# When the loads of the last stage are asked for: one in each of 17 steps, or one in each quarter of the last steps

## The chip, the cores and the metric

The kernel runs on one core of a Trainium2 chip (trn2). The metric is the device time of one execution in microseconds (us); the figure before is the median of three runs. All data is float32.

## The reference

The input x has 16 images of 64 channels of 128 × 128. Four layers follow, each of the form x = x + f(gn(x)), where gn is a group norm over groups of two channels:

- layer 0: the Gram matrix of an image's channels, applied to the image, then a product with a 64 × 64 matrix;
- layer 1: the absolute values of two Sobel-like 3 × 3 filters, added;
- layer 2: a shift of half of the channels by one column, then a 3 × 3 convolution of 64 to 64 channels with a bias;
- layer 3: a 3 × 3 convolution and a 1 × 1 convolution (done as one here), then a batch norm over all 16 images, a leaky ReLU and a clip to 0..255.

The batch norm matters for the shape of the kernel: its mean and variance need layer 3's product y of every image, so no element of the result can be finished before the last y is known.

## The kernel before, in words

Images go through a chain of four stages that work on different images at the same time: an image is cut into NS = 8 chunks (8 rows of each of its halves), and each stage works on one chunk in a step. A step has four quarters, q = 0 to 3. The loop runs over `steps` = 164 steps (0 to 163). `Gram` computes an image's Gram matrix; `Front` does layers 0 and 1; `Layer2` and `Layer3` do the convolutions. `starts` says how far the stages lie apart: for image b, Front's chunk 0 is at step 15 + 8b, Layer2's at 25 + 8b, Layer3's at 35 + 8b. For the last image (b = 15) Front ends at step 143, Layer2 has its last products in step 152, and Layer3 runs from step 155 (`last_one`) to 162, with a last store in 163. Layer3 of image 14 fills steps 147 to 154.

The order of instructions on each engine is the order in which the code records them (`InOrder`); no scheduler moves them. SP (SyncE) issues nearly all loads and stores, so an SP instruction that waits holds up all SP instructions behind it. Each SP load or store also waits, in the built program, until the one issued eight places earlier has landed.

What the steps around the change do on SP, in this order: in q = 1 Layer3 stores the y of the step before (`y_d<-y`, four stores of 128 KB), then Layer2 loads its chunk after the next (`v<-x_d`, six pieces, twelve for an image's last chunk); in q = 2 Layer2 stores its result, called x3 (`x_d<-x`, four stores of 128 KB). The names in the profile leave numbers out: y_d is layer 3's product in DRAM, x_d is layer 2's result (`x3_d`) or layer 1's (`x2_d`).

Buffers that later steps need: y has 2 (`ring`, tag "y"), x3 has NS + 2 = 10, v2 (layer 2's input) has 3. In q = 2 VectorE copies the product out of PSUM into y and adds the bias part c, `y<-two,c`; this needs a y buffer whose stores, two steps older, have landed. POOL copies the row differences d2 of layer 2 into a shifted twin, `qd<-d` (two pairs in a step, each a DMA issued by POOL on its own queue); TensorE reads them in q = 2 and q = 3. In layer 3 the twin is copied by ScalarE.

After the loop the end begins: the statistics (`mv`, `me_bn`, `var_bn`, `sc`, `sh`) are made from the sums, and then for each of 128 parts (512 KB of y, 512 KB of x3 and 512 KB of result each) ScalarE does the ReLU in place, VectorE the clip and the addition, and SP the store. The loads of a part are recorded by `fetch`, which takes two tiles of 128 × 1024 from a list of free places, `room`. Once the stages no longer need their tiles, `rest` and `slices` add them to `room`: `slices` cuts xw into 8 places, xh into 3, and d2 and its twin into one each; `rest` adds the tiles of a pool's tag. So some parts are fetched while the last steps still run, and three more after the loop:

```python
            yt, rt = room.popleft(), room.popleft()
            sp.dma_start(yt, whole(y_d[b], q))
            sp.dma_start(rt, whole(x3_d[b], q))
```

The fetched parts are the first ones, those of images 0 and 1, which were written long before. In the end, each part's places go back to `room`, and the next part is fetched into them.

Of the kernel before, what the change touches and what calls it, by code (L numbers as in the profile page):

```python
# [21 lines left out]
NS = HH // R  # L22
# [86 lines left out]
def tile_kernel(ctx: ExitStack, tc: tile.TileContext, x, cw_h, w2_t, b2, wbin_t, w1_t, b1, gamma, beta, consts, out):  # L109
# [142 lines left out]
    def tick():  # L252
        for c in list(chains):
            if next(c, chains) is chains:
                chains.remove(c)
# [608 lines left out]
    def run(stage, b, i, q):  # L864
        if 0 <= b < B and stage.first <= i <= stage.last:
            if (stage, b) not in live:
                live[stage, b] = stage(b)
            live[stage, b].at(i, q)
# [9 lines left out]
    last_one = NS * (B - 1) + starts[0][1]  # L878
# [5 lines left out]
    room, loaded = deque(), deque()  # L884
# [4 lines left out]
    def rest(pool, tag, shape, bufs, n=None):  # L889
        for m in range(bufs if n is None else n):  # L890
            t = pool.tile([P] + shape, F32, tag=tag, name=f"end_{tag}_{len(room)}", bufs=bufs)
            while len(t.shape) > 2:
                t = t.rearrange("p a b c -> p (a b) c" if len(t.shape) == 4 else "p a b -> p (a b)")
            room.append(t[:, 0:N])

    def slices(t, n):
        room.extend(t[:, j * N:(j + 1) * N] for j in range(n))
# [3 lines left out]
    def fetch():  # L901
        n = fetched[0]
        if n < len(parts):
            b, q = parts[n]
# [3 lines that stand above are left out]
            loaded.append((yt, rt))  # L908
            fetched[0] += 1

    for step in range(steps):
        for q in range(4):
            for b in range(B):

                i = step - starts[2][1] - NS * b
                if 0 <= i < NS and q in (0, 2):
                    live[Front, b].sobel(i, f"first of {q}")
                if q == 3:
                    run(Layer2, b, step - starts[1][1] - NS * b, "first of 3")
            for stage, at in starts:  # L920
                for b in range(B):
                    run(stage, b, step - at - NS * b, q)
            if q == 3:
                for b in range(B):
                    run(Layer2, b, step - starts[1][1] - NS * b, "last of 3")
            for b in range(B):
                at, n = pace[b]
                for m in range(n):
                    v = 4 * n * (step - at) + n * q + m
                    run(Gram, b, v // 4, v % 4)  # L930
            tick()

            if step == last_one and q == 0:
                slices(xw.rearrange("p w c t -> p (w c t)"), 8)
                slices(xh.rearrange("p a j w -> p (a j w)"), 3)
                rest(xin, "x", [R, W], 2)
                rest(xin, "xr", [C // 8, W], 3)
                rest(work, "u", [R + 1, W + 2], 2)
                rest(work, "e", [R, W + 2], 1)
                rest(ring, "v2", [(R + 1) * W + 2], 3)  # L940
                for t in (diffs["d2"], twins["d2"]):
                    slices(t.rearrange("p n j w -> p (n j w)"), 1)
            if step >= last_one and q == 2:

                n = 3 if step == last_one else 1 if step < last_one + NS - 2 else 0
                rest(ring, "x3", [2, CP, W], NS + 2, n)
            if step >= last_one and len(room) > 1:
                fetch()
    while chains:
        tick()  # L950
# [80 lines left out]
```

## Time and profile before

| | |
|---|---|
| median of three runs | 2827.53 us (2825.04 to 2830.61) |
| the profiled execution's own time | 2829.05 us |
| its span, from the first to the last instruction | 2827.3 us |
| TensorE, VectorE, ScalarE, GpSimd busy | 2241.5, 2200.4, 2120.5, 884.3 us |
| first ReLU of the end | at 2381.2 us of the span |
| end loads before the statistics | 16 parts (32 loads of 512 KB), first issued at 2299.6 us |
| DRAM read and written | 346.23 and 268.44 MB |

The page gives the busy time of each engine, then the span in 40 slices of 70.7 us with the busy share of each engine in tenths, the granted TensorE clock (PEclk) and the DMA engines' share and GB/s. The trace behind it gives the instructions of an engine in order of time: start, duration, instruction, and in square brackets how long the engine was idle before it and what ended that. Nearly all instructions carry line 73, that of the helper which records them, so they are told apart by the names of their tiles. Tiles that `rest` adds are called end_x, end_v and so on; xw, xh, d and qd are the same tiles as in the steps. A busy TensorE row has about 68 matmuls in 14 us in these steps.

### The profile page before, as it was taken

The page shows a single profiled execution, that of the slowest core. Times are in us where ns is not written, and L with a number is a line of the kernel's source. Part 1 is how long each engine was busy: PE and PEld are TensorE (multiplying, and loading weights), DVE is VectorE, ACT ScalarE, POOL GpSimd, SP SyncE. Part 2 cuts the span into 40 slices and gives each one's busy share as a digit, 9 for nine tenths or more (in the row PEclk, how much of TensorE's full clock was granted, in tenths as well). Part 3 has the DMA queues.
Part 4 walks back from the last instruction along what each step waited for, and adds up shares of the span by engine and source line. Part 5 has one row for each costly group of instructions (what it writes and reads, how often), then busy time and mean ns, then how long its engine had stood idle before and what let it go on. Part 6 is the DMA issues. An engine that isn't in the chain of part 4 may idle for free. (4 is left out here: it accounts for less than half of the span.)

```text
span 2827.3 us, 46297 instructions
## 1 busy us (share of the span) xinstructions
PE 2241.5 (79%) x14772; PEld 1157.1 (41%) x14772; DVE 2200.4 (78%) x3758; ACT 2120.5 (75%) x3171; POOL 884.3 (31%) x1326
## 2 busy tenths in 40 slices
PE   4568899999999999999999999999999995000000
PEld 2333444545453535363646363566666641000000
DVE  3999999898989898989898989999996434333332
ACT  4666779888888888888888888998997666333332
POOL 1035433343434343434343434454444300000000
PEclk8678999999999999999999999999999997555555
DMA  6788978888888888888888877888877668999999
GB/s 166 192 219 227 235 199 237 213 232 205 229 209 224 213 221 215 220 216 223 215 221 216 220 183 191 207 207 213 208 209 186 156 201 285 419 420 420 420 420 391
DMA packets 688880, 685.95 MB, mean 243 GB/s; under 512 B 61744, under 2 KB 590144, under 8 KB 688640
## 3 DMA queue, kind: packets, MB, share of 16 engines
q1 hardware_dynamic: 662656, 614.42, 73.7%
q0 software_dynamic: 24576, 68.12, 9.8%
q8 instruction: 119, 1.95, 0.3%
q14 instruction: 121, 0.99, 0.1%
q10 hardware_dynamic: 1408, 0.46, 0.1%
HBM read 346.23 MB, written 268.44 MB: 217 GB/s over the span
## 5 line engine op out<-in xcount | busy, mean ns | idle before, releaser
L73 PE MATMUL two<-d,w 128*64 128x508 f32 (+2 forms) x2560 | 894.2, 588 | 5.8 <-DVE d L73 5.8
L73 PE MATMUL two<-d,wi 128*64 128x508 f32 (+3 forms) x1536 | 620.1, 577 | 0.0
L73 POOL DMA_DIRECT2D qd<-d x512 | 269.8, 529 | 870.8 <-issue 318.4
L73 PE MATMUL two<-qd,pk 128*64 128x512 f32 (+1 forms) x1024 | 520.3, 589 | 3.2 <-DMA qd<-d 2.1
L73 POOL TENSOR_SCALAR edges<-v,co 64x8 f32<-64x8 f32 x512 | 348.8, 681 | 357.9 <-ACT v L73 248.7
L73 PEld LDWEIGHTS two<-d,w 128*64 128x64 f32 x2560 | 305.3, 136 | 285.5 <-issue 194.7
L73 PE MATMUL po<-x,abd 128*64 128x512 f32 x1024 | 369.8, 629 | 61.6 <-ACT xh L73 60.6
L73 DVE TENSOR_TENSOR d<-v 128x512 f32<-128x512 f32 (+1 forms) x512 | 345.9, 678 | 75.3 <-issue 36.0
L73 PE MATMUL one<-v,w 128*64 128x508 f32 (+2 forms) x1600 | 394.7, 578 | 0.0
L73 PE MATMUL one<-v,wi 128*64 128x508 f32 (+3 forms) x1536 | 391.4, 593 | 0.0
L73 ACT COPY qd<-d 64x512 f32<-64x512 f32 x512 | 315.3, 616 | 30.1 <-DVE d L73 23.7
L73 DVE SCALAR_TENSOR_TENSOR e<-e 128x1032 f32<-128x1032 f32 (+1 forms) x256 | 312.7, 1222 | 0.0
L73 ACT ACTIVATE xh<-po,co 128x128 f32<-128x128 f32 (+1 forms) x480 | 275.1, 621 | 40.8 <-PE po L73 38.8
L73 DVE SCALAR_TENSOR_TENSOR y<-two,c 128x1024 f32<-128x1024 f32 x128 | 155.8, 1217 | 132.0 <-ACT v L73 44.2
L73 PEld LDWEIGHTS two<-d,wi 128*64 128x64 f32 x1536 | 195.7, 136 | 145.2 <-issue 97.7
L73 POOL TENSOR_SCALAR v<-v,kc 128x9 f32<-128x9 f32 x256 | 249.7, 988 | 11.9
L73 PEld LDWEIGHTS one<-v,w 128*64 128x64 f32 x1600 | 171.9, 137 | 159.3 <-issue 97.5
L73 ACT ACTIVATE v<-x,co 128x512 f32<-128x512 f32 (+2 forms) x368 | 234.9, 704 | 0.0
L73 PEld LDWEIGHTS one<-v,wi 128*64 128x64 f32 x1536 | 163.0, 139 | 154.2 <-issue 110.1
L73 ACT ACTIVATE u<-u 128x1024 f32<-128x1024 f32 x128 | 135.5, 1058 | 96.7 <-DVE u L73 96.3
L73 DVE SCALAR_TENSOR_TENSOR u<-xh 128x1170 f32<-128x1170 f32 x128 | 175.5, 1371 | 12.2 <-ACT xh L73 9.8
L73 PEld LDWEIGHTS po<-x,abd 128*64 128x64 f32 x1024 | 110.8, 140 | 174.3 <-ACT xh L73 93.1
(154 smaller groups left out, 3476.0 us busy)
## 6 DMA issues: line engine op xcount, KB each, us to landing
xr<-in_x SPq DMA_DIRECT2D x128, 512.0 KB, 6.6
x<-in_x SPq DMA_DIRECT2D x256, 256.0 KB, 4.2
x_d<-u SPq DMA_DIRECT2D x512, 128.0 KB, 3.6
y_d<-y SPq DMA_DIRECT2D x512, 128.0 KB, 4.3
x_d<-x SPq DMA_DIRECT2D x496, 128.0 KB, 2.5
qd<-d POOLq DMA_DIRECT2D x256, 130.0 KB, 3.1
qd<-d POOLq DMA_DIRECT2D x256, 129.8 KB, 3.6
v<-x_d SPq DMA_DIRECT2D x448, 72.1 KB, 3.0
```

Of the source, the lines that this page charges most:

```text
L73: return self.tc.keep_in_program_order(call(*args, **kwargs))
```

## The change

Two things move. The tiles that Front and Gram leave (xw, xh, x, xr, u and e, 19 places) are put into `room` at step `last_one - NS` = 147 instead of `last_one` = 155; the tiles of Layer2 (v2 and d2 with its twin, 5 places) still at 155, and the x3 tiles as before. And `fetch` is called once in a step, in q = 3, from step 147 on, instead of in every quarter from step 155 on. Both wait for two free places (`len(room) > 1`).

```diff
-            if step == last_one and q == 0:
+            if step == last_one - NS and q == 0:
                 slices(xw.rearrange("p w c t -> p (w c t)"), 8)
                 slices(xh.rearrange("p a j w -> p (a j w)"), 3)
                 rest(xin, "x", [R, W], 2)
                 rest(xin, "xr", [C // 8, W], 3)
                 rest(work, "u", [R + 1, W + 2], 2)
                 rest(work, "e", [R, W + 2], 1)
+            if step == last_one and q == 0:
                 rest(ring, "v2", [(R + 1) * W + 2], 3)
                 for t in (diffs["d2"], twins["d2"]):
                     slices(t.rearrange("p n j w -> p (n j w)"), 1)
...
                 n = 3 if step == last_one else 1 if step < last_one + NS - 2 else 0
                 rest(ring, "x3", [2, CP, W], NS + 2, n)
-            if step >= last_one and len(room) > 1:
+
+            if step >= last_one - NS and q == 3 and len(room) > 1:
                 fetch()
```

The order of the parts and the places they go to stay the same, and so do the instructions of every engine other than SP and their order. On SP each of the 32 loads has another place in the order: the first fourteen stand between the x3 stores and the next y stores of steps 147 to 153, the rest behind the y stores of steps 154 to 162. The three fetches after the loop stay where they are.

## The prediction

> **What bounds the kernel now.** I read the page's 40 slices first (one slice is 70.7 us), then the busy time of each engine in stretches of 14 us around the steps that the change touches, then VectorE's and SP's instructions in order of time, then the chain of waits. The slices give the stages:
>
> ```profile
> PE   4568899999999999999999999999999995000000
> ...
> DMA  6788978888888888888888877888877668999999
> ```
>
> TensorE bounds the stepped part up to slice 34; the DMA engines bound the six slices after it, which are the end's loads and stores. Between them the stretches show a short piece where neither rule holds:
>
> ```profile
> 2232.00:2246.00 14.00, 14.00 (x68) 8.88 (x66) 5.65 (x11) 9.27 (x16) 4.87 (x10) 1.00 0.62 162
> ...
> 2316.00:2330.00 14.00, 14.00 (x61) 4.95 (x58) 4.88 (x8) 10.56 (x20) 0.00 (x0) 1.00 1.00 351
> 2330.00:2344.00 14.00, 11.50 (x42) 4.12 (x41) 2.44 (x4) 9.09 (x16) 0.00 (x0) 0.88 1.03 364
> 2344.00:2358.00 14.00, 10.58 (x39) 4.27 (x37) 2.44 (x4) 7.59 (x13) 0.00 (x0) 0.88 0.98 336
> 2358.00:2372.00 14.00, 13.73 (x58) 4.48 (x56) 4.88 (x8) 9.48 (x16) 0.00 (x0) 1.00 0.42 130
> ```
>
> The columns are PE, PEld, DVE, ACT, POOL (us busy, instructions), clock, DMA share, GB/s. At 2232 (step 149) TensorE is full and DMA has 38% free. From 2316 the DMA engines are full, and at 2330 TensorE loses time for the first time. Who holds it is seen in VectorE's copy of layer 3's product, one for each step:
>
> ```profile
> 2319.59 1.22 DVE L73 SCALAR_TENSOR_TENSOR y<-two,c 128x1024 f32<-128x1024 f32 x1 [5.38 <-ACT v L73]
> ...
> 2327.42 1.22 DVE L73 SCALAR_TENSOR_TENSOR y<-two,c 128x1024 f32<-128x1024 f32 x1 [5.38 <-PE two L73]
> ...
> 2338.32 1.22 DVE L73 SCALAR_TENSOR_TENSOR y<-two,c 128x1024 f32<-128x1024 f32 x1 [8.46 <-DMA y_d<-y]
> ...
> 2350.82 1.23 DVE L73 SCALAR_TENSOR_TENSOR y<-two,c 128x1024 f32<-128x1024 f32 x1 [10.06 <-DMA y_d<-y]
> ...
> 2360.07 1.23 DVE L73 SCALAR_TENSOR_TENSOR y<-two,c 128x1024 f32<-128x1024 f32 x1 [6.81 <-DMA end_x<-y_d]
> ...
> 2367.89 1.22 DVE L73 SCALAR_TENSOR_TENSOR y<-two,c 128x1024 f32<-128x1024 f32 x1 [5.38 <-ACT v L73]
> ...
> 2375.72 1.22 DVE L73 SCALAR_TENSOR_TENSOR y<-two,c 128x1024 f32<-128x1024 f32 x1 [5.39 <-issue]
> ```
>
> The last one is step 162, so these are steps 156 to 162. Three of them wait for a store of y (the third row names an end load, but the four DMA waits in the order of instructions are those of y's four stores): y has two buffers, so step 158 writes where step 156's y still lies. The store is late because SP issues it after eight end loads:
>
> ```profile
> 2324.32 0.43 SPq L73 DMA_DIRECT2D end_xr<-y_d  x1
> 2324.79 0.43 SPq L73 DMA_DIRECT2D end_xr<-x_d  x1
> 2325.27 0.43 SPq L73 DMA_DIRECT2D end_u<-y_d  x1
> 2325.74 0.70 SPq L73 DMA_DIRECT2D end_u<-x_d  x1
> 2326.76 4.48 SPq L73 DMA_DIRECT2D y_d<-y  x4
> ```
>
> The y of 2319.59 is stored from 2326.76, 6 us after it was ready, and lands behind full queues. Lastly the chain of waits, where the end starts:
>
> ```profile
> 2381.01 0.17 DVE sh L73
> 2381.18 0.03 issue
> 2381.21 1.25 ACT xw L73
> ...
> 2388.27 9.33 DMA out<-xh
> ```
>
> The batch statistics, which need the last y, gate the end at 2381.2; from 2388 on the chain is loads and stores of some 10 us each.
>
> **What the Trainium skill says.** (1) DMA: Bandwidth & Descriptors, section Anatomy of one DMA: "DMA engines do not wait on semaphores"; the issuing sequencer does. The trace agrees: SP's own waits name landings of xh, end_x, end_v and others between 2304 and 2358 (2.8 us for xh alone); while SP waits, the y store behind it is not issued. (2) Same page, section Queues, rings and completion order: each DMA engine takes turns between queue rows, packet by packet. So POOL's copies (queue q0) share with SP's loads (q1) rather than stand behind all of them; no view here shows this directly. (3) SBUF — State Buffer, section Who interferes with whom: DMA never contends with a compute engine. The trace agrees: the step of 7.83 us is the same at a DMA share of 1.00 (2319.59 to 2327.42) and of 0.42 (2367.89 to 2375.72). More DMA traffic alone costs the engines nothing here.
>
> **The change, part by part.**
>
> *Removed: bursts of end loads in steps 155 to 160.* An undisturbed step takes 7.83 us (2327.42 − 2319.59, and 2375.72 − 2367.89). The three disturbed ones take 10.90, 12.50 and 9.25 us: excess 3.08 + 4.68 + 1.43 = 9.2 us. The waits say the same: 8.46 + 10.06 + 6.81 = 25.3 us of idle VectorE, less 3 × 5.38 which it idles in any such step, is 9.2 us. This lies on the path: the last y, the statistics and the first end activation follow it. Gain 9.2 us.
>
> *Added there: one piece (two loads of 512 KB) in a step.* Its place on SP is right after the four y stores (2.6 us of issue when undisturbed), about 1.1 us more, in a step of 7.83. Per step DMA moves 1.05 MB of loads and 0.52 MB of stores: 1.57 MB at the 420 GB/s of the end is 3.7 us, under half the step. The next y store, 7.8 us later, finds the queues empty and lands in its usual 2.4 us; its buffer is wanted 15.7 us after the copy that filled it, and is free some 6.3 us after (1.2 + 2.6 + 2.4). Slack about 9 us, cost 0. The slots asked for were all released steps before (the tightest, x3's, two steps), so SP waits for none.
>
> *Moved into steps 147 to 153: seven pieces.* Six of these steps last 13.69 us (y copies at 2240.62 and 2254.30) with TensorE full; 153, without layer 2's products, is short. SP issues a piece right after the x3 stores, at 2238.2 in step 149, where it is idle until 2241.88: issue cost 0. The bytes are 1.05 MB, 2.5 us at 420 GB/s; the share of DMA rises from 0.62 to about 0.8 (0.62 + 2.5/13.69), as in 2092 to 2134, with batch 15's Front stage still running (0.76 to 0.85), where TensorE was also busy 14.00 of 14. What could be late:
> - POOL's twin copies of d2. The second is issued from 2236.60:
>
> ```profile
> 2236.60 1.03 POOL L73 DMA_DIRECT2D qd<-d  x2 [2.62 <-PE one L73]
> ...
> 2245.24 0.59 PE L73 MATMUL two<-qd,pk 128*64 128x512 f32 x1
> ```
>
> Landing takes a median of 2.9 us in these steps, so it is there at about 2240.5, 4.7 us before TensorE reads it. Even with the whole piece ahead of it, 2.2 us remain. The other twin lands before the piece is issued. In the fuller main loop their landing reached 6.9 us, and TensorE waited 3.3 us in all for them from 1501 to 2149.
> - v2's loads, issued at 2230.95 to 2234.9, are first used at 2252.35: 14 us of slack. x3 has ten buffers.
> - SP's issue limit: in the order of instructions each load or store of SP also waits for the one eight places before it. The third and fourth v2 load stand eight behind the piece. The piece, issued by 2239.3, must be in by 2245; at 2.5 us of transfer and some 2.4 us of landing it is in by about 2244. Even a miss of 3 us eats slack only.
>
> Cost 0; if the cover failed, up to 2.5 us a step. Bound from below: TensorE is full in those steps, so no gain.
>
> Pieces 8 and 9 fall in steps 154 and 155, then seven more up to step 162. Step 163 finds no room: 19 + 5 + 8 slots make 16 pieces, as before.
>
> *The end.* 16 pieces are in before the statistics either way, and three follow the loop right after the last y store. So 112 pieces are loaded (117.4 MB) and 128 stored (67.1 MB) in the end: 184.5 MB in 2379.7 to 2827.3, 412 GB/s. The same bytes in the same order, only 9.2 us earlier. In the new order the last piece is asked for 9 us before the statistics are ready, and it is the 16th to be used; no wait.
>
> *Sum.* −9.2 us: span 2827.3 to 2818.1, the profiled execution's own 2829.05 to 2819.9. Its time stands 1.5 us above the median of the runs, so the median goes from 2827.53 to 2818.3 (−0.33%).
>
> **Rivals.**
> - *A small price in each of the six steps* (landing on a twin, or SP's queue of eight), 0.6 to 1.5 us each, takes back 3.6 to 9 us: 2822 to 2827.5, within 0.2%, about what a measurement of this kernel can tell from no change. For it: the piece travels just while a twin does. Against it: the 4.7 us of slack.
> - *Slower: the twin waits for the whole piece, and TensorE with it.* If the slack were gone, each of the six steps would lose the piece's 2.5 us and some 0.5 us of the slower matmuls that follow a pause of TensorE (1.02 to 1.12 us instead of 0.59 from 2341.56 on): 6 × 3.0 − 9.2 = 8.8 us, 2836.3. It breaks even at 1.5 us a step and is slower by over 0.2% from 2.5 us. For it: TensorE has no idle time there to absorb it. Against: a twin's landing must go from 2.9 us to over 9 us before the gain is gone.
> - *No gain, since the end is bound by bytes.* Were DMA work conserved, an earlier start would only wait longer, 2827.5. Against: before 2381 DMA is idle half of the time (0.42 and 0.57 of the last two stretches), and the gate is the statistics.
> - *The loads do not spread as said* (a slot still held, SP blocked in front of a y store). Then some of the 3.08 to 4.68 us waits stay: 2821 to 2825. The order of instructions shows the spread, and the slots are long free.
>
> **How the numbers follow.** The forecast 0.84; price in the six steps 0.07; slower 0.04; conserved bytes 0.02; partly blocked 0.03 (half of it still faster by over 0.2%). Faster by over 0.2% (below 2821.9): 0.86; within: 0.10; slower: 0.04. Range: the three runs lie up to 2.5 us below and 3.1 above their median; 3.5 us below the forecast covers that with a microsecond for the reading of the undisturbed step, and 4.5 above it covers 3.1 and a price of 1.4 us: 2814.8 to 2822.8.
>
> **What would show it.** Right: copies of y every 7.83 us from step 155 to 162 with idle times of 5.4 us and no wait for y's store; steps 147 to 151 still 13.69 us with TensorE at 14.00 of 14; the first end activation near 2372.0; 446 us from there to the last instruction. Wrong: waits of TensorE for qd in 2210 to 2296, a step there over 14 us, or an end longer than 448 us.

## The result, and the profile after

The changed kernel takes 2819.53 us (median of 6 runs, 2816.38 to 2821.78), the kernel before, run beside it, 2828.14 us (6 runs). The ratio is 0.9969 with a 95% interval of 0.9959 to 0.9979: 8.8 us faster, with 5.9 to 11.6 as bounds. The forecast was 2818.3 us within 2814.8 to 2822.8. The profiled execution took 2818.68 us, its span 2816.9 us (forecast: 2819.9 and 2818.1).

The page of the changed kernel, TensorE and DMA in the 40 slices:

```profile
PE   4568899999999999999999999999999995000000
...
DMA  6789978888888888888888877787877767999999
```

TensorE's row is the same. In DMA's row the last slices before the end go from 7, 7, 6, 6, 8 to 7, 7, 7, 6, 7: slice 32 takes more, slice 34 less (156 and 285 GB/s before, 208 and 266 after). Finer, in stretches of 14 us (the columns as before: PE, PEld, DVE, ACT, POOL, clock, DMA share, GB/s):

```profile
2232.00:2246.00 14.00, 14.00 (x68) 6.29 (x66) 5.37 (x11) 9.21 (x15) 5.17 (x12) 1.00 0.78 225
...
2316.00:2330.00 14.00, 14.00 (x60) 4.83 (x60) 4.88 (x8) 10.59 (x18) 0.00 (x0) 1.00 0.62 201
2330.00:2344.00 14.00, 14.00 (x62) 4.99 (x59) 4.54 (x8) 10.59 (x19) 0.00 (x0) 1.00 0.69 209
2344.00:2358.00 14.00, 14.00 (x58) 4.74 (x57) 3.23 (x6) 12.15 (x21) 0.00 (x0) 1.00 0.73 224
```

At 2232 the DMA share went from 0.62 to 0.78 and TensorE is still busy 14.00 of 14. From 2316 the share is 0.62 to 0.73 instead of 0.98 to 1.03, and TensorE has no gap where it was busy 11.50 and 10.58. VectorE's copies of y in order of time, with the idle time ahead in brackets (steps 156, 158 to 160 and 162):

```profile
2318.44 1.23 DVE L73 SCALAR_TENSOR_TENSOR y<-two,c 128x1024 f32<-128x1024 f32 x1 [5.38 <-ACT v L73]
...
2334.08 1.22 DVE L73 SCALAR_TENSOR_TENSOR y<-two,c 128x1024 f32<-128x1024 f32 x1 [5.38 <-ACT v L73]
...
2341.90 1.22 DVE L73 SCALAR_TENSOR_TENSOR y<-two,c 128x1024 f32<-128x1024 f32 x1 [5.38 <-ACT v L73]
...
2349.72 1.22 DVE L73 SCALAR_TENSOR_TENSOR y<-two,c 128x1024 f32<-128x1024 f32 x1 [5.39 <-ACT v L73]
...
2365.37 1.22 DVE L73 SCALAR_TENSOR_TENSOR y<-two,c 128x1024 f32<-128x1024 f32 x1 [5.38 <-issue]
```

The copies lie 7.82 to 7.83 us apart in every step from 156 to 162, each with the idle time of an undisturbed step; the three waits of 8.46, 10.06 and 6.81 us are gone. SP in the same steps:

```profile
2319.70 2.58 SPq L73 DMA_DIRECT2D y_d<-y  x4
2322.44 0.49 SPq L73 DMA_DIRECT2D end_v<-y_d  x1
2323.10 0.33 SPq L73 DMA_DIRECT2D end_v<-x_d  x1
2327.52 2.58 SPq L73 DMA_DIRECT2D y_d<-y  x4
```

The y copied at 2318.44 is ready at 2319.6, and its stores are issued from 2319.70. Before, 6 us passed until then. From step 154 on, the y stores whose landing the trace holds (one or two of each four) took 2.4 us in the median and 3.7 at worst to land; before it was 5.2 in the median and 11.0 at worst. And the chain of waits where the end starts:

```profile
2370.67 0.17 DVE sh L73
2370.84 0.02 issue
2370.86 1.25 ACT xw L73
...
2382.01 8.65 DMA out<-end_x
```

The first end activation comes at 2370.86 instead of 2381.21, and from there to the last instruction it is 446.0 us in 2816.9, against 446.1 before.

### The profile page after: what moved, and what is told of

It reads as the page before. It is cut to its first block, busy times and chain, and to the rows that moved or that the text cites. A ratio compares the mean times of both kernels' runs of the same rounds, so it can differ in the third digit from the quotient of the medians.

```text
span 2816.9 us, 46299 instructions
## 1 busy us (share of the span) xinstructions
PE 2237.6 (79%) x14772; PEld 1153.6 (41%) x14772; DVE 2201.0 (78%) x3758; ACT 2121.1 (75%) x3171; POOL 887.5 (32%) x1326
## 5 line engine op out<-in xcount | busy, mean ns | idle before, releaser
L73 PEld LDWEIGHTS pg<-xw 128*64 128x64 f32 x4096 | 161.6, 143 | 46.4 <-issue 38.6
```

The costliest lines, as they stand in the source:

```text
L73: return self.tc.keep_in_program_order(call(*args, **kwargs))
```

## Where the 10.35 us of the two profiles lie

The two executions differ by 10.35 us at the first end activation, more than the forecast 9.2. The steps before the change's first moved load account for 1.47 us of it: the copy of y in step 146 lies at 2199.57 before and at 2198.10 after, and the first moved load is issued at 2209.33. Up to there the instructions and their order are the same, so that part is a difference between two executions, not a gain of the change. To read the others alike, time is counted below from that copy of step 146 to the first end activation ("gate"), and from there to the last instruction ("end").

| kernel | gate, us | end, us | median, us | ratio to before, 95% interval |
|---|---|---|---|---|
| before | 181.64 | 446.1 | 2827.28 to 2828.14 | |
| the change | 172.76 | 446.0 | 2819.53 | 0.9969 (0.9959 to 0.9979) |
| one piece in a step, from 155 | 172.46 | 465.9 | 2842.51 | 1.0047 (1.0034 to 1.0061) |
| two pieces in a step, from 155 | 172.45 | 446.5 | 2820.04 | 0.9970 (0.9959 to 0.9982) |
| bursts, third y buffer | 172.49 | 445.9 | 2820.98 | 0.9971 (0.9960 to 0.9983) |
| bursts from 147 | 173.55 | 446.0 | 2820.48 | 0.9976 (0.9967 to 0.9985) |
| bursts, y stores on POOL | 172.46 | 444.1 | 2819.89 | 0.9974 (0.9966 to 0.9983) |
| 18 pieces | 172.97 | 441.1 | 2816.59 | 0.9964 (0.9952 to 0.9976) |
| the change again | 172.46 | 446.1 | 2820.62 | 0.9978 (0.9970 to 0.9986) |

181.64 − 172.46 = 9.18 us is the excess that the prediction read off three steps. The change's own first profile has 0.3 us less of it (172.76): the step after 152 took 14.32 us instead of 14.11, and the six ahead 0.10 us more together. In the profile of the change taken again that is not there.

The gates agree more closely than the runs' times do. The change taken again is 6.2 us faster than before by its ratio, with 4.0 to 8.5 us as bounds, so 9.2 lies outside them; in the first measurement, 5.9 to 11.6, it lies inside. The time up to the copy of step 146, which the gate leaves out, varies from 2197.58 to 2202.03 us over the nine profiled executions. Whether the difference lies there is not shown: only one execution of each set of runs was profiled.

## The experiments

The theory: y's two buffers make VectorE wait for the stores of the step before last, and these are late because they stand behind several end loads on SP. The main rival: the DMA engines are full in steps 155 to 160, so the loads have to leave those steps.

**One piece in a step, but only from 155 on.** The spacing alone, without the earlier steps:

```diff
-            if step >= last_one and len(room) > 1:
+            if step >= last_one and q == 3 and len(room) > 1:
```

> The kernel before with the end's loads asked for in the last quarter of a step, one piece in a step, but still only from step 155 on (the places too). Theory (the y stores are late because SP has several pieces ahead of them): the copies of y come every 7.8 us from step 155 to 162, so the first end activation comes at about 2372, 9 us earlier than before; but only eight pieces are asked for before the last y instead of sixteen, so eight more are loaded in the end, 8 x 1.05 MB at 420 GB/s = 20 us: about 2839 us, 11 us slower than before. Rival (the end starts with DMA time to spare, so a piece not fetched early costs less than its 2.5 us): about 2820 to 2828 us. Rival (what counts is that loads leave steps 155 to 163 for earlier ones): the y waits stay, 2848 us.

Measured: 2842.51 us, 15 above before by the medians. The gate is 9.2 us earlier, as expected, and the end 19.8 us longer (expected: 20), since eight pieces more are left to it. Their sum, 10.6 us, lies inside the ratio's interval (9.6 to 17.2 us), though near its lower edge; the profiled execution was also 2.5 us late as early as step 146. The time is above the expected 2839 us, and both rivals are out: the waits for y are gone, and a piece that is not there when the end starts costs its 2.5 us in full. So spacing without enough steps to space over loses more than it gains.

**Two pieces in a step from 155 on.** The same 16 pieces, none ahead of step 155:

```diff
-            if step >= last_one and len(room) > 1:
+            if step >= last_one and q in (1, 3) and len(room) > 1:
```

> The kernel before with one piece in every second quarter (the second and the fourth) from step 155 on: two pieces in a step over eight steps, none moved ahead of step 155. DMA then has 2.1 MB of loads and 0.5 MB of stores in a step of 7.83 us, 335 GB/s, where the full stretches of before moved 336 to 364 GB/s. Theory (only the lateness of the y stores costs; a y buffer has some 9 us of slack): the stores come a few us late but inside the slack, 2819 to 2822 us, as the change. Rival (the pieces have to leave steps 155 to 162, since DMA is as good as full): part of the 9.2 us stays, 2823 to 2828 us.

Measured: 2820.04 us, the same as the change. One of its stretches, and a copy of y in it:

```profile
2330.00:2344.00 14.00, 14.00 (x58) 4.71 (x56) 3.23 (x7) 11.96 (x20) 0.00 (x0) 1.00 0.97 327
```

```profile
2343.91 1.22 DVE L73 SCALAR_TENSOR_TENSOR y<-two,c 128x1024 f32<-128x1024 f32 x1 [5.38 <-ACT v L73]
```

The DMA share is 0.97, and no step is held up; the y stores landed in 5.5 us at worst. So a DMA share near 1 is not by itself the cost, and the move to steps 147 to 154 is not needed for the gain. This takes the main rival away.

**The bursts left as they are, with a third y buffer in the last image.** The tile e of layer 1, which is no longer needed, serves as the third, and w2's tile gives the end's loads the place that e gave:

```diff
-                    y = ring.tile([P, 2, CP, W], F32, tag="y", name=f"y_{b}_{i}")
+                    if b == B - 1 and i % 3 == 2:
+                        y = work.tile([P, R, W + 2], F32, tag="e", name=f"y_{b}_{i}", bufs=1)
+                        y = flat(y)[:, 0:R * W].rearrange("p (s j w) -> p s j w", s=2, w=W)
+                    else:
+                        y = ring.tile([P, 2, CP, W], F32, tag="y", name=f"y_{b}_{i}")
...
-                rest(work, "e", [R, W + 2], 1)
+                slices(w2.rearrange("p s k o -> p (s k o)"), 1)
```

> The kernel before, its bursts of loads untouched, but with three buffers for y in the last image: every third y goes to the tile e of layer 1, and the place that e gave to the end's loads is taken from layer 2's weights w2, so there are as many pieces as before. Theory (the cost is the wait for y's buffers): the idle time of VectorE before y falls to 5.4 us in steps 158 to 160 or nearly so, the first end activation comes 7 to 9 us earlier, 2819 to 2822 us. Rival (full DMA engines or SP slow the steps in another way, the wait for y only shows it): 2826 to 2829 us, the steps stay at 9 to 12 us with another wait named.

Measured: 2820.98 us. Steps 158 and 159 in this kernel:

```profile
2336.84 1.23 DVE L73 SCALAR_TENSOR_TENSOR y<-two,c 128x1024 f32<-128x1024 f32 x1 [5.38 <-ACT v L73]
...
2344.66 1.23 DVE L73 SCALAR_TENSOR_TENSOR y<-two,c 128x1024 f32<-128x1024 f32 x1 [5.38 <-ACT v L73]
```

The y stores still land late (5.2 us in the median, 10.3 at worst), the DMA share is 1.03 and 1.04 in the two stretches from 2316 to 2344, and the gate gains the whole 9.2 us. At the gate the bursts cost the wait for y's buffers and nothing else that can be seen: it is 172.49 us with them and 172.46 without.

**The bursts left as they are, the last image's y stores issued by POOL.** Two buffers again, but another issuer:

```diff
-                            sp.dma_start(v[:, z], y[s * C:(s + 1) * C, z])
+                            (pool if b == B - 1 else sp).dma_start(v[:, z], y[s * C:(s + 1) * C, z])
```

> The kernel before, its bursts of loads untouched and y with two buffers, but the last image's y stores are issued by POOL, which is idle from step 153 on, on its own queue instead of SP's. Theory (the y stores are late because they stand behind SP's loads in SP's order): each store is issued as soon as its y is there and shares the DMA engines packet by packet, so it lands within some 6 us, inside the slack of 9; VectorE's idle time before y falls to 5.4 us in steps 158 to 160 and the time to 2818 to 2821 us. Rival (the DMA engines are full, so the stores land late whoever issues them): the waits of 8 to 10 us stay in part, 2823 to 2828 us.

Measured: 2819.89 us. A stretch of the burst in this kernel, then POOL in order of time, then the group of the y stores among the DMA issues (count, KB each, median us to landing):

```profile
2330.00:2344.00 14.00, 14.00 (x60) 4.77 (x58) 3.23 (x6) 11.68 (x20) 4.09 (x7) 1.00 1.03 411
```

```profile
2329.09 2.50 POOL L73 DMA_DIRECT2D y_d<-y  x4 [5.33 <-DVE y L73]
2336.92 2.50 POOL L73 DMA_DIRECT2D y_d<-y  x4 [5.33 <-DVE y L73]
```

```profile
y_d<-y POOLq DMA_DIRECT2D x28, 128.0 KB, 5.7
```

Here the DMA engines move 411 GB/s, more than the 364 of that stretch before, and SP's own loads of 512 KB take some 12 us to land. POOL issues a store as soon as its y is there, and it lands in 5.7 us. So the cost was not the load on the DMA engines but that the stores stood behind SP's loads.

They stood there in two ways, which this run removes together. First, the issue was late: the y of step 156, ready at 2320.82 in the kernel before, was issued from 2326.76. SP had eight loads to issue ahead of it and waited while doing so. The trace of the kernel before shows the limit of eight: in all 1212 cases in which it holds a landing, the SP transfer eight places later was issued only after that landing, while of those seven places later 237 were issued before it. Second, the landing was slow: a store of that y took 9.5 us from its issue. Eight loads of 512 KB are 4.2 MB, 10 us at the 420 GB/s of the end; this estimate comes near it. The slow landing alone cost nothing: the stores of step 155 were issued at once, took up to 11.0 us, and step 157's copy did not wait (5.38 us idle). How much of the later waits each of the two would leave alone, no run shows. The load on the engines is seen in the 5.7 us that POOL's stores take instead of 2.4, which the slack absorbs.

The end is 2 us shorter (444.1) too. SP, with no y store to wait for, asks for the first of the three pieces after the loop from 2357.79 on, ahead of the last y; that this is the reason was not tested.

**The change with bursts, from step 147 on.** This looks for the point at which the cover in layer 2's steps gives way:

```diff
-            if step >= last_one - NS and q == 3 and len(room) > 1:
+            if step >= last_one - NS and len(room) > 1:
```

> The changed kernel with a piece in every quarter from step 147 on instead of one in a step: nine pieces at once in steps 147 to 149, under layer 2, the rest from 155 on as places come free. Theory (in those steps the y buffers have 21 us of slack, v2's loads 14 us, and POOL's copies take turns with SP's loads): SP runs late by some 10 us, the six steps lose 0 to 5 us, and the smaller burst from step 155 loses 0 to 4 us: 2819 to 2825 us. Rival (a copy of POOL or a load of v2 stands behind the pieces and TensorE waits): steps 147 to 149 last over 15 us each, 2830 us or more.

Measured: 2820.48 us. The waits of TensorE from 2195 to 2300 now have a row that neither the change nor the kernel before has there:

```profile
PE two L73 <- DMA qd<-d: 0.5, 1, 0.5
```

The twins land in 4.6 us (median) and 8.4 (worst), against 2.9 and 4.4 in the kernel before. Step 148's copy of y comes 14.36 us after that of 147 instead of 13.68, and this wait is 0.5 us of the difference. With the other steps the price is 1.1 us (173.55 against 172.46). So the rival that TensorE waits for a twin behind the pieces is a real mechanism, but nine pieces in 39 us, under three steps, bring only one such wait. The change's one piece in a step leaves none. The y stores run late here too, one group from 2250.78 for a y that was ready at 2240.53, and no copy waits for them: in these steps of 13.7 us a y buffer is wanted some 26 us after its y is ready, where it is 14 from step 155 on.

**18 pieces instead of 16.** A version meant to beat both: four more places (w2; layer 2's wi, made 1 KB larger; a fourth place in a larger xh; the first 1024 columns of the constants, with bnavg moved behind them), and the fetches from step 145 on.

```diff
-            if step == last_one - NS and q == 0:
+            if step == last_one - NS - 2 and q == 0:
...
-                slices(xh.rearrange("p a j w -> p (a j w)"), 3)
+                slices(xhf, 4)
...
                 rest(ring, "v2", [(R + 1) * W + 2], 3)
+                slices(w2.rearrange("p s k o -> p (s k o)"), 1)
+                slices(kc, 1)
+                rest(stp, "wi", [R * W], 1)
...
-            if step >= last_one - NS and q == 3 and len(room) > 1:
+            if step >= last_one - NS - 2 and q == 3 and len(room) > 1:
```

> The changed kernel with four more free places (layer 2's weights w2, its tile wi made 1 KB larger, a fourth place in a larger xh, and the first 1024 columns of the constants, with the batch norm's matrix moved behind them), so that 18 pieces instead of 16 are asked for, one in each of steps 145 to 162. Theory (the end is bound by bytes from the first end activation on, 2.5 us for a piece of loads): the steps stay as they are and the end is 5 us shorter, 441 us from the first end activation to the last instruction: 2814 to 2815 us. Rival (steps 145 and 146, with the Front stage's last stores near, or the end's order take it back): 2818 to 2821 us.

Measured: 2816.59 us (5 runs, 2815.47 to 2817.47). The end is 441.1 us in the profile (expected: 441); the gate is 0.5 us later than in the best of the others, most of it in step 154 (8.19 us instead of 7.81). The median is above the expected 2814 to 2815 us and below the rival's 2818 to 2821. It is 4.0 us below the change taken again, and 67 of the 70 pairs of one run of each have the 18 pieces faster; the two intervals against the kernel before (0.9952 to 0.9976, 0.9970 to 0.9986) overlap a little. Shown is the shorter end, and that this version is very likely the faster of the two; by how much is not settled.

**The change again**, unaltered, on the same chip as the runs with the y stores on POOL and with 18 pieces:

> The changed kernel itself, unaltered, beside the two others on the same chip: 2817 to 2821 us by every theory; it is what the run with 18 pieces is to be compared with.

Measured: 2820.62 us (14 runs, 2817.03 to 2824.97). Its gate is 172.46 us.

## Why the prediction was right, point by point

- **The excess of three steps, 9.2 us on the path.** Right: in four kernels that remove the late stores or their effect each in its own way, and in the second profile of the change, the gate falls by 9.15 to 9.19 us (8.88 in the change's first profile). That it was the buffers' wait (third buffer) and that standing behind SP's loads made it (POOL) is shown, each by a run that leaves the bursts. That the first measurement of the change, 2819.53 us, lies so near to the forecast of 2818.3 is in part luck: its gain is known to within some 3 us either way, and the second measurement gave less.
- **One piece in a step costs nothing in steps 154 to 162.** Right: 7.82 us a step, stores landing in 2.4 us.
- **Six pieces under layer 2 cost nothing.** Right to within 0.3 us, and 0 in the second profile. The DMA share came to 0.78 in step 149's stretch, 0.84 in the second profile (forecast: about 0.8). The twins landed in 3.0 us in the median and 5.3 at worst, in place of 2.9 and 4.4. The worst is 2.4 us more than the usual landing, about the time of the whole piece, and uses half of the 4.7 us of slack.
- **The end is the same 446 us.** Right. Its pricing by bytes was tested in both directions: eight pieces more gave 19.8 us (2.5 us each), two fewer gave 5.0 us.
- **The rivals.** Conserved bytes: excluded, the gate moved and the end did not grow. A slot still held: every y store was issued as soon as its y was there. The wait for a twin: exists, at a dose that the change does not give.
- **Of the Trainium skill's three statements** two were tested further. DMA: Bandwidth & Descriptors, section Queues, rings and completion order, has the engines take turns between queue rows by packets; no view showed it then. POOL's stores, 5.7 us beside SP's loads of some 12 us, fit it, without showing the turns themselves. SBUF — State Buffer, section Who interferes with whom: steps of 7.82 to 7.83 us at a DMA share of 1.03 (y stores on POOL) and at 0.62 (the change) agree with it.
- **What the prediction had wrong in its reasons,** without harm to its sum. It treated the move ahead of step 155 as part of what brings the gain. Two pieces in a step from 155 on bring the same. The earlier steps are needed only if a step gets a single piece: from 155 on alone, that leaves eight pieces for the end. It put the transfers of a step from 154 on at 3.7 of 7.83 us, a share of 0.47; the bytes came as forecast (201 to 224 GB/s from 2316 to 2358), but the share was 0.62 to 0.73. And TensorE did not lose time for the first time at 2330: the stretch from 2302 to 2316, which it does not show, has 13.50 us busy of 14 in the kernel before and in the change, so that loss is not what the change removes.

## What to carry to other kernels

When a prefetch shares an in-order queue with the stores that free a working buffer, look at how many bytes the queue puts ahead of one such store, not at the DMA share, and compare the time they take with the slack of the buffer. Here eight loads in a row made it too late, four were inside the slack (5.5 us to land at worst), and a second issuer or a third buffer did as well as spreading. And if the stage that follows is bound by bytes, a prefetch counts only if it is done before that stage opens: space the loads, but over enough steps that none is left over.

## What the runs showed that was not expected

A DMA share near 1 did not say that the DMA engines were at their limit. With two pieces in a step the share was 0.97 at 327 GB/s, in the kernel before 1.03 at 364 GB/s, and with the y stores on POOL 1.03 at 411 GB/s, each in the stretch from 2330 to 2344. The share counts the time that packets took, and here they took longer or shorter for the same bytes. In these runs the rate, set against the 420 GB/s of the end, was the better guide to what still fitted.
